# Combining expert outputs with diagonal matmuls, normalizing on ScalarE, and taking the c_fc_2 products pair by pair, in a two-layer vision kernel

## The chip, the cores and the metric

The kernel runs on one core of one Trainium2 chip. The metric is the device time of one launch in microseconds (us). It is told as the median of several runs; three runs of the kernel before gave 4483.56 us (4473.93 to 4485.39). One more execution was recorded by the hardware profiler; all durations below come from it. Engines are named as in the profile: PE is the matrix engine (PEld its weight loads), DVE the vector engine, ACT the scalar engine, POOL the general engine, SP the engine that only issues DMAs.

## The reference, cut to what matters

The input x has shape (4, 384, 32, 32): 4 batches, 384 channels, 1024 positions. All arithmetic is float32.

```python
x = x + scan_conv(ln_c(x))               # selective scan in 4 directions, then layernorm and gelu
t = tokens(x)                            # (4, 1024, 384)
t = t + experts(ln_t(t))                 # 4 experts, the best 2 for each token, weighted by their gates
x = from_tokens(t)
x = x + attention(ln_c(x))               # 8 heads of 64, output projection w_out, bias b_out
t = tokens(x)
t = t + kron_ffn(ln_t(t))                # h = gelu(n @ kron(c_fc_1, c_fc_2).T); h @ kron(c_proj_1, c_proj_2).T
...
def ln(v, eps): return (v - mean(v)) / sqrt(var(v) + eps)
out = einsum('bse,ebsd->bsd', masked_gates, y)      # the weighted sum of two experts' rows
```

kron(c_fc_1, c_fc_2) has 32 blocks of 12 channels: the product with c_fc_2 is an elementwise product of a token with a tiled row of 384 numbers, followed by a sum over each group of 12. The kernel does it before it subtracts the mean and scales, which it does on the 32 sums.

## The kernel before, in words

**Scan layer** (`scan_layer`, lines 192 to 291). For each of 4 batches there are 4 directions times 2 halves of 512 positions; each such unit has 3 chunks of 128 channels, each 4 groups of states. Per group POOL multiplies twice at L420 and once at L448 (128x1024 each), ACT makes the decays at L429, DVE runs 4 scans at L434 and 2 products at L441, and PE sums over states at L455. When a batch ends, `finish` normalizes (`layernorm`, lines 150 to 188, two halves), applies gelu and adds the input.

**Tail of a batch.** `route` and `spread` (lines 601 to 664) make tokens out of channels, take the statistics, compute gates and places (`places`), normalize each token block (L649) and scatter each row to two places in DRAM with indirect DMAs from POOL's queue (L654). `experts` (lines 807 to 902) runs 11 slots of 256 or 128 rows, each with one expert's weights: matmuls at L879, gelu at L888, matmuls at L895, an add of the bias on DVE (L899), and a DMA from SP's queue that writes the rows to `made` (L900). `combine` (lines 904 to 926) gathers for each of 8 blocks of 128 tokens the two rows `got` (L913, 16 indirect DMAs from POOL's queue), ACT multiplies each by its gate into PSUM (L920), and DVE adds both to the token block `xt` (L924). `xt` is written to DRAM (L925). `prologue` (lines 930 to 944) takes statistics (`stats`, lines 516 to 527), normalizes `xt` in place (L531), transposes on PE (L939) and copies to `xc` on ACT (L943). `attention` (lines 946 to 1047) follows, and then `last_layers` (lines 1049 to 1156): output projection (L1083) in four pairs of token blocks, added to `xt` by DVE (L1087); statistics; the product with c_fc_2 (L1091) and its sums over 12 (L1093) for all 8 blocks at once; the transposed result `z`; hidden matmuls, gelu (L1128), the second product and the output.

**Inverse roots.** In `layernorm` (L178), `stats` (L525) and `spread` (L636) ACT takes a Sqrt, `exp_again` (lines 141 to 144) loads the table of Exp and Ln back, and DVE takes the reciprocal (L180, L526, L637).

**What sets the order.** Every engine runs its instructions in the order of its queue. The order is made before the launch by a list scheduler that simulates the kernel with its own durations (line 1285); `high_priority(offset=FORWARD)` moves `combine`, `prologue`, `last_layers` and `spread` ahead of what else is ready. The tails of batches 0 and 1 and the experts of batch 2 run beside the scans of the batches after them; the rest of batch 2's tail and the whole tail of batch 3 run when the last scan has ended, at about 3555 us of the span.

**Buffers.** Tails 0 to 2 use the room `t` and batch 3 the room `w`, with the numbers of buffers per tag given here. `two()` hands out the tag "s" of PSUM (two banks), which the combine, the transposes, the hidden matmuls, the scores and the output projection share; `bank("o")` and `bank("p")` are single banks.

```python
NARROW = {"kw": 8, "k12": 2, "k4": 5, "got": 1, "bb": 2}
WIDE = {"kw": 10, "k12": 3, "k4": 4, "got": 2, "bb": 2}
NARROW_BANKS = {"s": 1, "o": 1, "p": 1}
WIDE_BANKS = {"s": 2, "o": 2, "p": 2}
```

Batch 3 has the narrow banks up to the end of `prologue`, and the wide ones from its attention on. `second_layer_exact` is inside a condition that does not hold for this input; the trace has none of its instructions.

Of the kernel before, what the change touches and what calls it, by code (L numbers as in the profile page):

```python
# [12 lines left out]
ALU = mybir.AluOpType  # L13
# [101 lines left out]
class Body:  # L115
# [29 lines left out]

    def col(self, name, i):
        at = COL[name][0] + i
        return self.cols[:, at : at + 1]

    def layernorm(self, src, dst, eps, psum, work):  # L150

        nc = self.nc
        for i in range(NH):
            sl = halves(i)
            mean = psum.tile([P, HF], F32, tag="ps", name="ln_mean")
            for c in range(DC):
# [12 lines left out]
            var = psum.tile([P, HF], F32, tag="ps", name="ln_var")  # L169
            for m in range(nm):  # L170
                for c in range(DC):
                    nc.tensor.matmul(
                        var[:, m : m + 1], sqs[c][:, m * P : (m + 1) * P], self.ones[:, :1],
                        start=(c == 0), stop=(c == DC - 1),
                    )
            std = work.tile([P, nm], F32, tag="ln_std", name="ln_std", bufs=2)
            self.exp_again(
                nc.scalar.activation(std, var[:, :nm], AF.Sqrt, bias=eps, scale=1.0 / D).ins  # L178
            )
            nc.vector.reciprocal(std, std)  # L180
# [304 lines left out]
    def first_layer(self, b, room):  # L485

        self.experts(b, self.slots, room)
        with self.tc.high_priority(offset=FORWARD):
            xt = self.combine(b, *self.place, room)
            return self.prologue(xt, xt, room)  # L490
# [25 lines left out]
    def stats(self, xt, eps, room):  # L516
# [8 lines left out]
        self.exp_again(nc.scalar.activation(rstd, mv[:, :, 1], AF.Sqrt, bias=eps).ins)  # L525
        nc.vector.reciprocal(rstd, rstd)  # L526
        return mv[:, :, 0], rstd

    def normalize(self, xt, mean, rstd, out):
        for m in range(MB):  # L530
            self.nc.vector.tensor_scalar(  # L531
                out[:, m, :], xt[:, m, :], mean[:, m : m + 1], rstd[:, m : m + 1],
                op0=ALU.subtract, op1=ALU.mult,
            )
# [71 lines left out]
    def spread(self, b, x1, room):  # L606
# [29 lines left out]
        self.exp_again(nc.scalar.activation(rstd, mv[:, :, 1], AF.Sqrt, bias=self.eps5).ins)  # L636
        nc.vector.reciprocal(rstd, rstd)  # L637
        nc.vector.tensor_mul(sc, sc, rstd.unsqueeze(2).to_broadcast([P, MB, NE]))
        nc.vector.tensor_add(sc, sc, self.bg.unsqueeze(1).to_broadcast([P, MB, NE]))
        pos, gate, expert = self.places(sc, room)  # L640
# [166 lines left out]
    def experts(self, b, routed, room):  # L807
# [57 lines left out]
        for s in range(NSLOT):  # L865
# [34 lines left out]
            nc.sync.dma_start(  # L900
# [3 lines left out]
    def combine(self, b, pos, gate, room):  # L904

        nc = self.nc
        xt = room.tile([P, MB, D], "k12", "xt")
        nc.sync.dma_start(out=xt, in_=self.tokens(b))
        got = []
# [7 lines left out]
        for m in range(MB):  # L917
            ps = room.two("w_ps")
            for k in range(TOP):
                nc.scalar.activation(  # L920
                    ps[:, k, :D], got[m][:, k, :], AF.Copy, scale=gate[:, k, m : m + 1]
                )
            for k in range(TOP):
                nc.vector.tensor_add(xt[:, m, :], xt[:, m, :], ps[:, k, :D])  # L924
        nc.sync.dma_start(out=self.tokens(b), in_=xt)  # L925
        return xt
# [3 lines left out]
    def prologue(self, xt, xn, room):  # L930

        nc = self.nc
        mean, rstd = self.stats(xt, self.eps6, room)
        self.normalize(xt, mean, rstd, xn)
        xc = room.tile([P, DC, L], "k12", "xc")
        for c in range(DC):
            ps = room.two("tc_ps")
            for m in range(MB):
                nc.tensor.transpose(  # L939
                    ps[:, m // 4, m % 4 * P : (m % 4 + 1) * P], xn[:, m, c * P : (c + 1) * P],  # L940
# [108 lines left out]
    def last_layers(self, b, att, room):  # L1049
# [27 lines left out]
        nc.gpsimd.tensor_add(xt, xt, bout.unsqueeze(1).to_broadcast([P, MB, D]))  # L1077
        for m in range(0, MB, 2):
# [8 lines left out]
            nc.vector.tensor_add(xt[:, m : m + 2, :], xt[:, m : m + 2, :], ps[:, :, :D])  # L1087

        mean, rstd = self.stats(xt, self.eps5, room)
        prod = room.tile([P, MB, D], "k12", "prod")  # L1090
        nc.vector.tensor_mul(prod, xt, c2.unsqueeze(1).to_broadcast([P, MB, D]))  # L1091
        zt = room.tile([P, MB, KR], "zt", "zt")
        nc.vector.tensor_reduce(  # L1093
            zt.rearrange("p m r -> p (m r)"), prod.rearrange("p m (r j) -> p (m r) j", j=KJ),
            AX.X, ALU.add,
        )
# [61 lines left out]
    def second_layer_exact(self):  # L1158

        nc, tc, a = self.nc, self.tc, self.a  # L1160
        with ExitStack() as ctx:
# [10 lines left out]
            for b in range(B):  # L1172
                xc = work.tile([P, DC, L], F32, tag="xc", name="xc", bufs=1)
                att = work.tile([P, HEADS // 2, L], F32, tag="att", name="att", bufs=1)
                with ExitStack() as part:
# [4 lines left out]
                    nc.vector.tensor_copy(xc, self.prologue(xt, xt, room))  # L1180
# [205 lines left out]
```

## Time and profile before

| | |
|---|---|
| median of 3 runs | 4483.56 us |
| the profiled execution's own time | 4517.48 us |
| its span, first to last instruction | 4513.6 us |
| mean granted TensorE clock | 0.831 |
| PE busy | 3440.6 us (76%) |
| DVE busy | 3010.8 us (67%) |
| POOL busy | 3037.0 us (67%) |
| ACT busy | 2534.3 us (56%) |
| 16 DMA engines, queue of SP | 50.3% |

The profile's page gives for each engine its busy share in 40 slices of the span (112.8 us each, in tenths), then the costliest groups of instructions: line, engine, operation, output<-inputs, shapes, count, busy us and mean ns, then the time that the engine stood idle just before them and what ended it. The timeline view lists instructions in order of time: start, duration, engine, line, and in brackets the idle time before and who ended it. The view by stages gives the busy time of each engine in a stretch of time.

### The profile page before, as it was taken

To read this page: it belongs to the slowest core of one execution; us is meant where nothing else is said; L and a number is where in the kernel's file an instruction comes from. 1 tells how busy PE (TensorE), PEld (TensorE's weight loads), DVE (VectorE), ACT (ScalarE), POOL (GpSimd) and SP (SyncE) were. 2 spreads that over 40 slices of the span, in tenths; PEclk is the share of its full clock that TensorE was granted. 3 is DMA by queue.
4 is the path that set the end of the run, shared out by engine and by line. 5 is a ranking of instruction groups with operands and counts; after the bars stand their busy time and mean duration, and the time that the engine had idled before them with its cause. 6 is when DMAs were issued, how large, how long until landed. Compare 5 with 4: busy or idle time off the path is not lost. (4 is left out here: it accounts for less than half of the span.)

```text
span 4513.6 us, 46925 instructions
## 1 busy us (share of the span) xinstructions
PE 3440.6 (76%) x13852; PEld 1652.0 (37%) x13852; DVE 3010.8 (67%) x4344; ACT 2534.3 (56%) x4406; POOL 3037.0 (67%) x1467
## 2 busy tenths in 40 slices
PE   6545554479894787669998588757998689999796
PEld 2111121145552222225555222214555445556333
DVE  4999997878878977977877777896778520002102
ACT  4555554456665676466666577556666444334554
POOL 4999998788987877778988778878889510000100
PEclk7666665589996898669998699858999789999897
DMA  4444554477886533457779443445787543344200
GB/s 119 118 123 118 146 136 106 137 230 209 231 240 181 149 84 104 130 159 226 210 220 275 137 114 101 115 139 170 232 244 232 169 157 115 107 127 153 75 16 15
DMA packets 404361, 684.81 MB, mean 152 GB/s; under 512 B 50944, under 2 KB 206464, under 8 KB 404096
## 3 DMA queue, kind: packets, MB, share of 16 engines
q1 hardware_dynamic: 395360, 656.16, 50.3%
q0 software_dynamic: 8192, 25.17, 1.7%
q8 instruction: 111, 1.82, 0.2%
q14 instruction: 154, 1.26, 0.1%
q10 hardware_dynamic: 544, 0.40, 0.0%
HBM read 561.47 MB, written 120.06 MB: 151 GB/s over the span
## 5 line engine op out<-in xcount | busy, mean ns | idle before, releaser
L420 POOL TENSOR_TENSOR bx<-dtr,bcs 128x1024 f32<-128x1024 f32 x768 | 1797.8, 2366 | 227.7 <-PE acc L455 103.5
L429 ACT ACTIVATE da<-dtr,nega 128x512 f32<-128x512 f32 x1536 | 1045.5, 691 | 1039.4 <-DVE bx L441 569.0
L448 POOL TENSOR_TENSOR bx<-bx,bcs 128x1024 f32<-128x1024 f32 x384 | 903.6, 2358 | 211.8 <-DVE bx L434 88.0
L455 PE MATMUL acc<-bx,sel 128*32 128x512 f32 x3072 | 511.8, 713 | 312.4 <-POOL bx L448 248.8
L879 PE MATMUL h_ps<-xc,w 128*128 128x256 f32 (+1 forms) x3168 | 680.1, 370 | 61.7 <-DVE xc L861 31.5
L895 PE MATMUL y_ps<-w,hs 128*128 128x384 f32 x1824 | 649.9, 509 | 49.8 <-ACT hs L888 44.1
L879 PEld LDWEIGHTS h_ps<-xc,w 128*128 128x128 f32 x3168 | 557.2, 200 | 253.4 <-issue 120.4
L434 DVE TENSOR_TENSOR_SCAN bx<-da,carry,bx 128x512 f32<-128x512 f32 x384 | 474.0, 1269 | 118.6 <-POOL bx L420 65.5
L434 DVE TENSOR_TENSOR_SCAN bx<-da,bx 128x512 f32<-128x512 f32 x384 | 452.2, 1209 | 129.2 <-POOL bx L420 70.3
L434 DVE TENSOR_TENSOR_SCAN da<-da,carry,bx 128x512 f32<-128x512 f32 x384 | 476.5, 1273 | 67.9 <-ACT da L429 62.6
L441 DVE TENSOR_TENSOR bx<-da,bcs 128x512 f32<-128x512 f32 x768 | 509.8, 679 | 3.8
L434 DVE TENSOR_TENSOR_SCAN da<-da,bx 128x512 f32<-128x512 f32 x384 | 456.3, 1218 | 60.7 <-ACT da L429 44.2
L895 PEld LDWEIGHTS y_ps<-w,hs 128*128 128x128 f32 x1824 | 352.3, 198 | 341.7 <-issue 86.4
L992 ACT ACTIVATE ex<-s_ps 128x512 f32<-128x512 f32 x512 | 299.4, 591 | 274.9 <-PE s_ps L987 259.9
L987 PE MATMUL s_ps<-w 64*128 64x512 f32 x1024 | 308.4, 674 | 83.1 <-ACT ex L992 74.2
L1077 POOL TENSOR_TENSOR xt<-xt,wb 128x3072 f32<-128x3072 f32 x4 | 26.8, 6708 | 477.5 <-DMA w<-in_w 345.5
L1036 PE MATMUL o_acc<-ex,vt 128*64 128x512 f32 x1024 | 295.6, 658 | 0.8 <-ACT att L1044 0.8
L455 PEld LDWEIGHTS acc<-bx,sel 128*32 128x32 f32 x3072 | 77.7, 117 | 596.0 <-POOL bx L448 363.8
L884 ACT ACTIVATE hs<-h_ps,bb 128x256 f32<-128x256 f32 (+1 forms) x528 | 194.0, 447 | 128.8 <-PE h_ps L879 128.5
L899 DVE TENSOR_TENSOR y<-y_ps,bb 128x384 f32<-128x384 f32 x76 | 41.6, 548 | 237.6 <-PE y_ps L895 237.6
L913 POOL DMA_INDIRECT got<-made,g_pos x64 | 60.8, 950 | 192.4 <-PE f_acc L1136 159.1
L987 PEld LDWEIGHTS s_ps<-w 64*128 64x128 f32 x1024 | 81.1, 192 | 266.8 <-ACT ex L992 149.1
(216 smaller groups left out, 4021.9 us busy)
## 6 DMA issues: line engine op xcount, KB each, us to landing
w<-in_w SPq DMA_DIRECT2D x352, 576.0 KB
dtr<-dd SPq DMA_DIRECT2D x1536, 128.0 KB
bcs<-rows SPq DMA_DIRECT2D x512, 128.0 KB
dd<-one_e SPq DMA_DIRECT2D x96, 256.0 KB
dd<-mag SPq DMA_DIRECT2D x96, 256.0 KB
rows<-zero SPq DMA_DIRECT2D x76, 192.0 KB
xs<-rows SPq DMA_DIRECT2D x32, 384.0 KB
made<-y SPq DMA_DIRECT2D x32, 384.0 KB
```

The costliest lines, as they stand in the source:

```text
L420: pool = nc.gpsimd.tensor_mul(bx, dtr[q][1], bc[:, 0].unsqueeze(1).to_broadcast([P, 2, HF])).ins
L429: nc.scalar.activation(da, dtr[q][0][:, j, :], AF.Exp, scale=nega[:, col : col + 1])
L434: nc.vector.tensor_tensor_scan(run(h), run(da), run(bx[:, j, :]), 0.0 if first else hold, ALU.mult, ALU.add,)
L441: dve = nc.vector.tensor_mul(bx[:, j, :], h, cg).ins
L448: pool = nc.gpsimd.tensor_mul(bx, bx, cg.unsqueeze(1).to_broadcast([P, 2, HF])).ins
L455: nc.tensor.matmul(acc[lo : lo + DB, :], sel, out[q][:, j, :], start=(g == 0), stop=(g == NG - 1),)
L879: nc.tensor.matmul(ps[:, r, :], w1[(f + r) // wf][:, c, (f + r) % wf * P : ((f + r) % wf + 1) * P], xc[:, c, :], start=(c == 0), stop=(c = ...
L884: nc.scalar.activation(hs[:, f + r, :], ps[:, r, :], AF.Identity, bias=bb[:, f + r : f + r + 1])
L895: nc.tensor.matmul(out[:, :D], hs[:, f, t * P : (t + 1) * P], w2[f // wf][:, f % wf, :], start=(f == 0), stop=(f == FC - 1),)
L987: nc.tensor.matmul(ps[:, o, :], w[rows, j * P : (j + 1) * P], w[rows, halves(i)], start=True, stop=True,)
L992: ins = nc.scalar.activation(ex[:, o, :], ps[:, o, :], AF.Exp, scale=HD**-0.5, accum_out=sums[:, t, 2 * j + o, i : i + 1],).ins
L1036: ins = nc.tensor.matmul(out[cols, :], made[t][1][:, j, cols], ex[:, o, :], start=(j == 0), stop=(j == MB - 1),).ins
```

## The change

The inverse root becomes exp(-0.5 ln(var + eps)), two ACT instructions with one table. `combine` makes two tensors of 8 diagonal matrices from the gates on POOL, and PE multiplies them with the gathered rows and sums both experts in PSUM; DVE adds a pair of blocks at once. `normalize` is gone: ACT applies scale and bias (`less` is minus mean times the inverse root) and writes, in `combine`'s case, into the first half of `got`. The last slot's rows are written to `made` from ACT's queue instead of SP's. In `last_layers` the product with c_fc_2 and its sums are taken after each pair of the output projection, with the product in the pair's PSUM tile.

```diff
+    def inverse_root(self, out, var, eps, scale=1.0):
+        self.nc.scalar.activation(out, var, AF.Ln, bias=eps, scale=scale)
+        self.nc.scalar.activation(out, out, AF.Exp, scale=-0.5)
...
# layernorm (and stats with mv[:, :, 1], eps; and spread with self.eps5)
-            self.exp_again(
-                nc.scalar.activation(std, var[:, :nm], AF.Sqrt, bias=eps, scale=1.0 / D).ins
-            )
-            nc.vector.reciprocal(std, std)
+            self.inverse_root(std, var[:, :nm], eps, scale=1.0 / D)
...
-    def normalize(self, xt, mean, rstd, out):
-        for m in range(MB):
-            self.nc.vector.tensor_scalar(
-                out[:, m, :], xt[:, m, :], mean[:, m : m + 1], rstd[:, m : m + 1],
-                op0=ALU.subtract, op1=ALU.mult,
-            )
+    def less_mean(self, mean, rstd, room, tag):
+        less = room.tile([P, MB], tag, "less")
+        self.nc.vector.scalar_tensor_tensor(less, mean, -1.0, rstd, op0=ALU.mult, op1=ALU.mult)
+        return less
...
# spread (less is taken before self.places)
-            nc.vector.tensor_scalar(
-                xt[:, m % 2, :], xt[:, m % 2, :], mv[:, m, :1], rstd[:, m : m + 1],
-                op0=ALU.subtract, op1=ALU.mult,
+            nc.scalar.activation(
+                xt[:, m % 2, :], xt[:, m % 2, :], AF.Identity,
+                bias=less[:, m : m + 1], scale=rstd[:, m : m + 1],
             )
...
# experts
-            nc.sync.dma_start(
+            queue = nc.sync if s + 1 < NSLOT else nc.scalar
+            queue.dma_start(
                 out=made[at : at + size, :].rearrange("(t p) d -> p t d", p=P), in_=y
             )
...
# combine
+        diag = []
+        for k in range(TOP):
+            d = room.tile([P, MB, P], "k4", "diag")
+            nc.gpsimd.tensor_mul(
+                d, self.ident.unsqueeze(1).to_broadcast([P, MB, P]),
+                gate[:, k, :].unsqueeze(2).to_broadcast([P, MB, P]),
+            )
+            diag.append(d)
...
-        for m in range(MB):
+        for m in range(0, MB, 2):
             ps = room.two("w_ps")
-            for k in range(TOP):
-                nc.scalar.activation(
-                    ps[:, k, :D], got[m][:, k, :], AF.Copy, scale=gate[:, k, m : m + 1]
-                )
-            for k in range(TOP):
-                nc.vector.tensor_add(xt[:, m, :], xt[:, m, :], ps[:, k, :D])
+            for o in range(2):
+                for k in range(TOP):
+                    nc.tensor.matmul(
+                        ps[:, o, :D], diag[k][:, m + o, :], got[m + o][:, k, :],
+                        start=(k == 0), stop=(k == TOP - 1),
+                    )
+            nc.vector.tensor_add(xt[:, m : m + 2, :], xt[:, m : m + 2, :], ps[:, :, :D])
         nc.sync.dma_start(out=self.tokens(b), in_=xt)
-        return xt
+        return xt, [got[m][:, 0, :] for m in range(MB)]
...
# prologue
         mean, rstd = self.stats(xt, self.eps6, room)
-        self.normalize(xt, mean, rstd, xn)
+        less = self.less_mean(mean, rstd, room, "less")
+        for m in range(MB):
+            nc.scalar.activation(
+                xn[m], xt[:, m, :], AF.Identity, bias=less[:, m : m + 1], scale=rstd[:, m : m + 1]
+            )
...
# last_layers, after each pair of the output projection
+            pair = xt[:, m : m + 2, :]
+            nc.vector.tensor_add(pair, pair, ps[:, :, :D])
+            nc.vector.tensor_mul(ps[:, :, :D], pair, c2.unsqueeze(1).to_broadcast([P, 2, D]))
+            for o in range(2):
+                nc.vector.tensor_reduce(
+                    zt[:, m + o, :], ps[:, o, :D].rearrange("p (r j) -> p r j", j=KJ),
+                    AX.X, ALU.add,
+                )
         mean, rstd = self.stats(xt, self.eps5, room)
-        prod = room.tile([P, MB, D], "k12", "prod")
-        nc.vector.tensor_mul(prod, xt, c2.unsqueeze(1).to_broadcast([P, MB, D]))
...
-        nc.vector.tensor_reduce(
-            zt.rearrange("p m r -> p (m r)"), prod.rearrange("p m (r j) -> p (m r) j", j=KJ),
-            AX.X, ALU.add,
-        )
```

More of the change, by code (lines that the diff above doesn't have):

```diff
@@ L488, in first_layer @@
         with self.tc.high_priority(offset=FORWARD):
-            xt = self.combine(b, *self.place, room)
-            return self.prologue(xt, xt, room)
+            xt, xn = self.combine(b, *self.place, room)
+            return self.prologue(xt, xn, room)
     def second_layer(self, b, xc, room, between):
@@ L524, in stats @@
             nc.vector.bn_aggr(mv[:, m, :], st[:, m, :])
-        self.exp_again(nc.scalar.activation(rstd, mv[:, :, 1], AF.Sqrt, bias=eps).ins)
-        nc.vector.reciprocal(rstd, rstd)
+        self.inverse_root(rstd, mv[:, :, 1], eps)
         return mv[:, :, 0], rstd
-    def normalize(self, xt, mean, rstd, out):
-        for m in range(MB):
-            self.nc.vector.tensor_scalar(
-                out[:, m, :], xt[:, m, :], mean[:, m : m + 1], rstd[:, m : m + 1],
-                op0=ALU.subtract, op1=ALU.mult,
-            )
+    def less_mean(self, mean, rstd, room, tag):
+        less = room.tile([P, MB], tag, "less")
+        self.nc.vector.scalar_tensor_tensor(less, mean, -1.0, rstd, op0=ALU.mult, op1=ALU.mult)
+        return less
     def moe_consts(self, room):
@@ L635, in spread @@
             nc.sync.dma_start(out=self.tokens(b)[:, m : m + 2, :], in_=xt)
-        self.exp_again(nc.scalar.activation(rstd, mv[:, :, 1], AF.Sqrt, bias=self.eps5).ins)
-        nc.vector.reciprocal(rstd, rstd)
+        self.inverse_root(rstd, mv[:, :, 1], self.eps5)
         nc.vector.tensor_mul(sc, sc, rstd.unsqueeze(2).to_broadcast([P, MB, NE]))
         nc.vector.tensor_add(sc, sc, self.bg.unsqueeze(1).to_broadcast([P, MB, NE]))
+        less = self.less_mean(mv[:, :, 0], rstd, room, "r_less")
         pos, gate, expert = self.places(sc, room)
@@ L939, in prologue @@
                 nc.tensor.transpose(
-                    ps[:, m // 4, m % 4 * P : (m % 4 + 1) * P], xn[:, m, c * P : (c + 1) * P],
+                    ps[:, m // 4, m % 4 * P : (m % 4 + 1) * P], xn[m][:, c * P : (c + 1) * P],
                     self.ident,
@@ L1077, in last_layers @@
         nc.gpsimd.tensor_add(xt, xt, bout.unsqueeze(1).to_broadcast([P, MB, D]))
+        zt = room.tile([P, MB, KR], "zt", "zt")
         for m in range(0, MB, 2):
@@ L1086, in last_layers @@
                     )
-            nc.vector.tensor_add(xt[:, m : m + 2, :], xt[:, m : m + 2, :], ps[:, :, :D])
-        mean, rstd = self.stats(xt, self.eps5, room)
-        prod = room.tile([P, MB, D], "k12", "prod")
-        nc.vector.tensor_mul(prod, xt, c2.unsqueeze(1).to_broadcast([P, MB, D]))
-        zt = room.tile([P, MB, KR], "zt", "zt")
-        nc.vector.tensor_reduce(
-            zt.rearrange("p m r -> p (m r)"), prod.rearrange("p m (r j) -> p (m r) j", j=KJ),
-            AX.X, ALU.add,
-        )
+            pair = xt[:, m : m + 2, :]
[6 more added lines that the diff above has]
+                )
+        mean, rstd = self.stats(xt, self.eps5, room)
         shift = room.tile([P, MB], "shift", "shift")
@@ L1179, in second_layer_exact @@
                     nc.sync.dma_start(out=xt, in_=self.tokens(b))
-                    nc.vector.tensor_copy(xc, self.prologue(xt, xt, room))
+                    xn = [xt[:, m, :] for m in range(MB)]
+                    nc.vector.tensor_copy(xc, self.prologue(xt, xn, room))
                 with ExitStack() as part:
```

## The prediction

> **What bounds the kernel now.** I read the profile's page first, the engines' busy share in 40 slices:
>
> ```profile
> PE   6545554479894787669998588757998689999796
> DVE  4999997878878977977877777896778520002102
> ...
> POOL 4999998788987877778988778878889510000100
> ```
>
> Up to slice 31 (about 3550 us) DVE and POOL run the scan, nearly full while nothing else runs (slices 1 to 5) and at 7 to 9 tenths once the tails run beside it. Then both fall idle and PE works alone. So there are two limits. The groups say why POOL and DVE are so close:
>
> ```profile
> L420 POOL TENSOR_TENSOR bx<-dtr,bcs 128x1024 f32<-128x1024 f32 x768 | 1797.8, 2366 | 227.7 <-PE acc L455 103.5
> ...
> L448 POOL TENSOR_TENSOR bx<-bx,bcs 128x1024 f32<-128x1024 f32 x384 | 903.6, 2358 | 211.8 <-DVE bx L434 88.0
> ```
>
> Per group of states POOL has 3 such instructions, 7.1 us; DVE has four scans of 1.24 us and two products of 0.68 us, 6.3 us, plus copies and its share of the tails. Neither is the limit alone; what the tails put on DVE comes back in part.
>
> For the part after the scan I read the timeline, since the chain of waits reaches back only to 3043 us. The view by stages of the two combines there (batch 2 beside the scan's last layernorm, batch 3 before its attention), with columns PE, PEld, DVE, ACT, POOL, clock, DMA, shows that no engine is full in either:
>
> ```profile
> 3553.00:3609.00 56.00, 21.71 (x83) 16.29 (x82) 24.34 (x54) 27.57 (x36) 22.56 (x22) 0.57 0.49 154
> 4184.00:4249.00 65.00, 38.62 (x184) 20.89 (x184) 20.05 (x44) 34.67 (x40) 15.20 (x16) 0.72 0.40 124
> ```
>
> They are chains of waits. The timeline of batch 3's:
>
> ```profile
> 4208.38 0.95 POOL L913 DMA_INDIRECT got<-made,g_pos  x1 [0.30 <-issue]
> ...
> 4213.89 1.14 DVE L924 TENSOR_TENSOR xt<-xt,w_ps 128x384 f32<-128x384 f32 x2 [11.47 <-ACT w_ps L920]
> ...
> 4231.50 1.14 DVE L924 TENSOR_TENSOR xt<-xt,w_ps 128x384 f32<-128x384 f32 x2 [0.46 <-ACT w_ps L920]
> ...
> 4238.43 3.20 DVE L531 TENSOR_SCALAR xt<-xt,mv,rstd 128x384 f32<-128x384 f32 x8 [2.35 <-DMA x<-xt]
> ```
>
> The last gather is issued at 4209.33, but the last add ends at 4232.64: one PSUM tile goes back and forth between ACT and DVE, and ACT's queue also holds the copies and gelus of batch 2's last layers. Then the normalization waits 2.35 us because it overwrites a tile that a DMA still reads.
>
> At the end, DVE alone, with PE idle 10.9 us:
>
> ```profile
> 4439.10 3.34 DVE L1091 TENSOR_TENSOR prod<-xt,wb 128x3072 f32<-128x3072 f32 x1
> ...
> 4442.51 3.32 DVE L1093 TENSOR_REDUCE zt<-prod 128x256 f32<-128x3072 f32 x1
> ...
> 4446.47 1.43 DVE L1102 TENSOR_TENSOR z<-zt,rstd 128x256 f32<-128x256 f32 x4
> ```
>
> **The change part by part.** All of it stands against this profiled execution (4517.48 us, span 4513.6), which is 34 us above the median of the three runs; I take the difference off the median.
>
> *Scan stage, DVE* (occurrences before 3550 us). Gone: 32 adds of L924 at 0.55 (17.7 us); the normalizations L531 of batches 0 and 1 (11.4 + 5.2 us; undisturbed they take 3.2 each) and L649 of batches 0 to 2 (30.4 less 3.4 of batch 3, 27.0 us); the product and sums L1091 and L1093 of batches 0 and 1 (30.6 less 13.3 of the others, 17.3 us); some 21 reciprocals (4 us). Sum 82.6 us. New: 8 adds of 768 at 0.95 (row L1087), 7.6; 8 products of 768 into PSUM at about 0.95 (same row), 7.6; 16 sums of 384 at 0.48 (L1093: 3.32 us for 3072, so 0.415 for 384, plus some 0.06 of start), 7.7; 5 `less` at 0.2 (row L638), 1.0. Sum 23.9 us. DVE gets 58 us lighter (82.6 less 23.9 is 58.7).
>
> L531 and L649 are long only in the scan stage: eight took 11.41 us at 1443 us, of which one alone 8.69, while POOL ran three products in a row, against 0.40 each at 4238. The new product also has both inputs in SBUF: L1102, another such, took 2.55 us for four at 1878 us and 1.43 at 4446, and L638 took 2.34 beside POOL and 0.19 without it. So each of the 8 products may wait 0 to 2.2 us, at most 17 us in all; I take 3, since L1102's four lost about 1.1 us together.
>
> The Trainium skill ("SBUF — State Buffer", section "Who interferes with whom") states this as a lock: a DVE instruction with two SBUF inputs, or in a 2-port mode as a tensor_scalar can be, blocks fully against a POOL instruction that reads SBUF, and a reduction never does. It speaks for moving L531 and L649 and against cutting one product into four, since each piece can meet the lock; by the rule the pieces cost up to 17 us, by the row about 3.
>
> *Scan stage, ACT.* 21 Sqrts go, each with a table load before and after: 42 x 1.283 = 53.9 us, and 5.8 us for themselves; 32 products L920 at 0.58, 18.7 us. New: 21 times Ln at 0.3 (a 128x8 Sqrt takes 0.30) and Exp at 0.23 (row of 128x32), 11 us; 40 normalizations of 384 at about 0.6 (L920 with one pointer operand 0.58; L362 with 512 columns 0.72), 24 us. ACT gets 43 us lighter. It isn't the limit, but DVE's scans waited 212 us for its decays.
>
> The Trainium skill ("ScalarE: Activation LUTs", section "What ACT_TABLE_LOAD costs") puts a switch at about 2.66 us, with a drain behind the load. Here the drain does not show: at 4234.24 a load of 1.28 us is followed by its Sqrt at 4235.54. By the rule ACT would gain some 58 us more; I stay with the row.
>
> *Scan stage, POOL.* Two diagonal products per batch, 128x1024 from two SBUF inputs: 2.36 us each by L420, 6 of them, 14.2 us on a queue that is nearly the limit; bounds 0 (if they land in one of POOL's waits) and 14. They sit in its queue before the gathers and need two "k4" buffers of the last expert slots; if the queue gets to them early, the products behind them wait.
>
> *Scan stage, PE.* 16 products of 384 columns per batch; L895's records take 0.51 us, two each, so 16 us a batch, which lie under the gathers (16 issues, 1.25 us apart, 20 us).
>
> Sum for the scan stage: DVE 58 less 3, of which I count half since POOL stands beside it (-28), POOL +14: **-14 us**. Ends: all of DVE's and nothing of POOL's, -58; nothing of DVE's, all of POOL's and of the lock, +31.
>
> *Combine of batch 2* (3553 to 3609). The last gather is issued by 3576.0 and lands 2.2 us later (the first of batch 3 is issued by 4188.76 and used at 4190.94). Then one product (1.0), one add (0.95) and two statistics (1.5) end at 3581.7; now they end at 3602.0. The inverse root is 0.7 us instead of 0.3 + 0.2, but without loads; the normalization starts at once instead of 5.5 us later, since it writes another tile, and takes 8 x 0.6 = 4.8 instead of 3.2 us. `xc` is 23 us earlier. What that is worth: from 3700 us PE is full to 4184 with experts of batch 3 and attention of batch 2; the lead pays only where PE is idle, and between 3600 and 3700 it is busy 77.5 us. So 0 to 22 us; I take half, **-11 us**. In the last layernorm (L178) the load already hides behind the variance matmuls: nothing there.
>
> *Combine of batch 3.* In the same way the statistics end at 4215, not 4233.5, and `xc` is some 21 us earlier. But batch 2's last layers share PE and ACT, hold the narrow banks until their output (4240.5) and, at the same gather times, need about 7 us for a hidden block, 4 for its gelu, twice, 4 for the product and 8 for the output from 4187, so 4223 at best. Ends 0 and -21; I take **-15 us**, as ACT loses the 16 products between them.
>
> *Last layers of batch 3.* Per pair PE takes 5.16 us; DVE's add, product, two sums and statistics take 0.95 + 0.95 + 0.96 + 1.3 = 4.2 us, so three pairs hide. After the last add (4438.1) come 3.2 us, then 0.6 of mean and shift: z starts at 4442.1, not 4446.5: **-4 us** (-3 to -5). The cover is PE's; with one bank, as in batches 0 to 2, the pair's tile is held about 2 us longer, but there PE has experts to run.
>
> *The last write of `made` from ACT's queue.* In batches 0, 2 and 3 SP issued it 0.02 to 0.03 us after the add, so nothing is gained. ACT must wait for that add: behind it stand the scan's decays. An issue on ACT took 0.45 us (L203). Ends 0 and +4 (a bias add's wait of some us in each batch); I take 0.
>
> Sum: 14 + 11 + 15 + 4 = 44 us off 4483.56: **4440 us**.
>
> **The rivals.**
> *All of it couples* (chance 0.08): DVE's 55 us and both leads of 21 come through: -58 - 22 - 21 - 5 = -106 at the extreme, some -90 likely, 4394. For it: DVE and ACT wait for each other 917 us at L429. Against: POOL's own 2702 us.
> *The leads are not used* (0.17): batch 2's last layers hold batch 3, and PE's idle time is waiting for `places`, not for `xc`. Only 14 + 4 remain: 4465. For it: POOL waited 56.2 us for the places before the scatter.
> *POOL decides the scan* (0.12): the diagonals cost 14, DVE's relief nothing; with half the leads, +14 - 13 - 4 = -3: 4480, no change.
> *PE's queue takes over the wait* (0.15): a combine's matmul waits for its gather at the head of PE's queue, and behind it stand the scan's sums L455, the last layernorm's matmuls and batch 2's hidden blocks. First issue to last landing is 23.7 us (4187.8 to 4211.5). Held for 20 us in batches 0, 1 and 2, and batch 3's lead lost, it costs 60 against 14 + 11 + 4: +31, 4515. It decides from about 10 us per combine (three of them against 29). For it: POOL already waited 103.5 us for L455. Against: POOL issues gathers for 20 us in that stretch and feeds the scan nothing, so PE has little to do.
>
> **How the numbers follow.** The forecast's own case has 0.48. A measurement here tells 0.3%, 13 us, from no change. Faster: 0.48 + 0.08 + 0.17 = 0.73; same 0.12; slower 0.15. The range 4400 to 4490 leaves out most of the first and of the last rival, about 0.19. All queues are laid out anew by a planner; that may add either sign, and is why I keep the range this wide.
>
> **What would show it.** Right: the last add of batch 3's combine within 5 us of its last landing; no table load at Sqrt; L649's and L531's place taken by ACT at 0.55 to 0.65 us each; z within 5 us of the last pair's add; the scan's end some 14 us earlier than 3550. Wrong: PE idle on gathers with L455 or L172 behind; POOL waiting at the diagonals; the scan's end later than now.

## The result, and the profile after

The changed kernel took 4527.01 us (median of four runs, 4524.48 to 4532.37), the kernel before on the same chip 4478.75 us (4472.73 to 4485.39). The ratio is 1.0109, 95% interval 1.0089 to 1.0129: slower by about 48 us, and above the predicted range. The profiled execution took 4532.37 us, its span is 4530.6 us, the mean granted clock 0.842.

The page of the changed kernel, the same three engines in 40 slices:

```profile
PE   5554554549997888669998687768999699999797
DVE  4888888778887866978886766888788730020002
...
POOL 3899988778898867788998766879899821000100
```

In slices 1 to 5 (113 to 680 us), where nothing but the scan of batch 0 runs, DVE has fallen from 9 to 8 tenths, and POOL shows two 8s where it had only 9. Both engines do the same scan work there, so something makes them wait. POOL's costliest groups (busy, mean, idle before and what ended it):

```profile
L422 POOL TENSOR_TENSOR bx<-dtr,bcs 128x1024 f32<-128x1024 f32 x768 | 1794.4, 2362 | 270.4 <-PE acc L457 145.7
...
L450 POOL TENSOR_TENSOR bx<-bx,bcs 128x1024 f32<-128x1024 f32 x384 | 904.3, 2359 | 243.6 <-DVE carry L447 108.0
```

They are as long as before, and the idle time ahead of them is larger, 514.0 us instead of 439.5. The reason stands in ACT's groups for the first 900 us. First the kernel before:

```profile
L144 ACT ACT_TABLE_LOAD x8 | 10.3, 1283 | 0.1
L178 ACT ACT_TABLE_LOAD x6 | 7.7, 1283 | 4.6 <-PE ln_var L172 4.6
...
L636 ACT ACT_TABLE_LOAD x1 | 1.3, 1283 | 0.0
```

Then the changed kernel:

```profile
L355 ACT ACT_TABLE_LOAD x27 | 34.6, 1283 | 4.2 <-DMA dd<-one_e 3.3 <-PE dt_ps L360 0.4
L431 ACT ACT_TABLE_LOAD x25 | 32.1, 1283 | 0.4
L148 ACT ACT_TABLE_LOAD x6 | 7.7, 1283 | 4.6 <-PE ln_var L177 4.6
L149 ACT ACT_TABLE_LOAD x6 | 7.7, 1283 | 0.1
L353 ACT ACT_TABLE_LOAD x2 | 2.6, 1283 | 0.0
```

With the single loads of both lists, 69 loads now against 17 before. L355 is the scan's Ln and L431 its Exp: lines that the diff does not touch. ACT's timeline of the changed kernel (start, duration) shows how they take the table from each other:

```profile
308.90 1.28 ACT L355 ACT_TABLE_LOAD   x1
310.19 0.63 ACT L355 ACTIVATE lnw<-one_e 128x512 f32<-128x512 f32 x1
310.85 0.63 ACT L357 ACTIVATE one_e<-one_e 128x512 f32<-128x512 f32 x1
311.50 1.28 ACT L431 ACT_TABLE_LOAD   x1
312.79 1.30 ACT L431 ACTIVATE da<-dtr,nega 128x512 f32<-128x512 f32 x2
```

In the kernel before, `exp_again` stood behind each Sqrt, and the first of them, in batch 0's first layernorm, loaded the set of tables that holds Exp and Ln together. The change removes it there. ACT's timeline of the kernel before, then of the changed kernel, at that place:

```profile
19.70 1.28 ACT L178 ACT_TABLE_LOAD   x1 [4.56 <-PE ln_var L172]
21.00 0.26 ACT L178 ACTIVATE ln_std<-ln_var,eps 128x4 f32<-128x4 f32 x1
21.28 1.28 ACT L144 ACT_TABLE_LOAD   x1
```

```profile
19.93 1.28 ACT L148 ACT_TABLE_LOAD   x1 [4.56 <-PE ln_var L177]
21.22 0.26 ACT L148 ACTIVATE ln_std<-ln_var,eps 128x4 f32<-128x4 f32 x1
21.51 1.28 ACT L149 ACT_TABLE_LOAD   x1
22.80 0.20 ACT L149 ACTIVATE ln_std<-ln_std 128x4 f32<-128x4 f32 x1
```

L144 is `exp_again`; L148 and L149 are the Ln and the Exp of the new root. Nothing else asks for that set before the `exp_again` behind the first gelu, at 853 us; until then each Ln and each Exp is given a set that lacks the other. Start of the scan layer's gelu, batch by batch:

| | batch 0 | 1 | 2 | 3 | span |
|---|---|---|---|---|---|
| before | 791 | 1731 | 2674 | 3592 | 4513.6 |
| after | 849 | 1788 | 2756 | 3683 | 4530.6 |
| after, with one load of the joint set at the start (the first run below) | 789 | 1728 | 2695 | 3616 | 4464.2 |

58 us are lost before the first gelu. Against the third row, 60 us are lost there and 66 at the end: they are not won back. Against the kernel before, the distance grows to 91 us at batch 3 and shrinks to 17 at the end: from the scan's last sum to the end it takes 878 us instead of 960, and the profiled execution of the kernel before was a long one, 34 us above its median. What the change promised for the combine is there too. The changed kernel's timeline of DVE, end of batch 3's combine (the last gather is issued by about 4250):

```profile
4253.35 0.95 DVE L937 TENSOR_TENSOR xt<-xt,w_ps 128x768 f32<-128x768 f32 x1 [2.14 <-PE w_ps L933]
4254.34 1.02 DVE L525 BATCH_NORM_STATS2 st<-xt 128x6 f32<-128x384 f32 x2
4255.28 0.30 DVE L526 BATCH_NORM_AGGREGATE mv<-st 128x2 f32<-128x6 f32 x2
4256.19 0.17 DVE L533 SCALAR_TENSOR_TENSOR less<-mv,rstd 128x8 f32<-128x8 f32 x1 [0.61 <-ACT rstd L149]
```

The last add ends 4.9 us after the last gather's start; it was 24.3. And batch 3's last pair of the output projection:

```profile
4458.88 0.95 DVE L1107 TENSOR_TENSOR xt<-xt,o_ps 128x768 f32<-128x768 f32 x1 [1.21 <-PE o_ps L1102]
...
4463.67 1.43 DVE L1121 TENSOR_TENSOR z<-zt,rstd 128x256 f32<-128x256 f32 x4
```

`z` starts 3.8 us after the last add ends, where it was 8.3.

### The profile page after: what moved, and what is told of

The parts are those of the page before. It is cut to its first block, busy times and chain, and to the rows that moved or that the text cites. A ratio compares the mean times of both kernels' runs of the same rounds, so it can differ in the third digit from the quotient of the medians.

```text
span 4530.6 us, 47195 instructions
## 1 busy us (share of the span) xinstructions
PE 3496.9 (77%) x13980; PEld 1660.7 (37%) x13980; DVE 2977.3 (66%) x4252; ACT 2555.5 (56%) x4446; POOL 3051.1 (67%) x1475
## 5 line engine op out<-in xcount | busy, mean ns | idle before, releaser
L422 POOL TENSOR_TENSOR bx<-dtr,bcs 128x1024 f32<-128x1024 f32 x768 | 1794.4, 2362 | 270.4 <-PE acc L457 145.7
L431 ACT ACTIVATE da<-dtr,nega 128x512 f32<-128x512 f32 x1536 | 1044.3, 690 | 1046.2 <-DVE bx L443 610.3
L879 PE MATMUL h_ps<-xc,w 128*128 128x256 f32 (+1 forms) x3168 | 669.3, 366 | 50.4 <-DVE xc L861 25.8
L916 POOL TENSOR_TENSOR diag<-ident,g_picked 128x1024 f32<-128x1024 f32 x8 | 15.0, 1894 | 274.3 <-DMA out<-out 261.1
L347 PE MATMUL dt_ps<-xd,wdt 12*128 12x512 f32 x192 | 127.2, 747 | 69.0 <-ACT mag L386 31.6
```

What stands on the lines that cost most here:

```text
L422: pool = nc.gpsimd.tensor_mul(bx, dtr[q][1], bc[:, 0].unsqueeze(1).to_broadcast([P, 2, HF])).ins
L431: nc.scalar.activation(da, dtr[q][0][:, j, :], AF.Exp, scale=nega[:, col : col + 1])
L879: nc.tensor.matmul(ps[:, r, :], w1[(f + r) // wf][:, c, (f + r) % wf * P : ((f + r) % wf + 1) * P], xc[:, c, :], start=(c == 0), stop=(c = ...
```

## The experiments

Each run is told as a ratio to runs of the kernel before that were made beside it, since the kernel before itself took 4479.6, 4511.3, 4477.7 and 4513.9 us beside the four groups of runs, the last two on the same chip. Letters in the expectations: T, the table loads cost what was lost, against R, the other parts did; P, each part has the price that its own instructions show, against Q, the order of the queues decides; W, the wait for `less`, against O, the order. The expectations also call PE TensorE, DVE VectorE, ACT ScalarE and POOL GpSimd. Line numbers shift a little from kernel to kernel.

**First group: the tables.** One line added to the changed kernel, `e1_after_preload`:

```diff
-            nc.scalar.activation(nega, self.cols[:, lo:hi], AF.Exp)
+            self.exp_again(nc.scalar.activation(nega, self.cols[:, lo:hi], AF.Exp).ins)
```

> The changed kernel with one table load more: right behind the first Exp (nega) the table that holds both Exp and Ln is loaded. Theory T (tables): in batch 0 no instruction loads that table any more, so Ln and Exp take it from each other some 50 times up to 850 us; with the load the loads at L353, L355 and L431 vanish, the first gelu of the scan layer comes back from 846 us to about 790 us, and the kernel takes 4465 to 4485 us, level with the kernel before (4479) or below it. Rival R (DVE's waits for POOL at the small products and the new order): at most 10 us come back, over 4515 us.

Measured 4466.19 us, ratio 0.997 (0.9958 to 0.9981), 61 us under the changed kernel. Its loads in the first 900 us are four, of which the joint set is loaded at L144:

```profile
L144 ACT ACT_TABLE_LOAD x2 | 2.6, 1283 | 0.0
L208 ACT ACT_TABLE_LOAD x1 | 1.3, 1283 | 1.7 <-PEq L1397 1.7
L230 ACT ACT_TABLE_LOAD x1 | 1.3, 1283 | 0.0
```

The queues of PE, DVE, POOL and SP hold the same instructions in the same order in both kernels, and ACT's differ by loads only: a clean pair, two kernels whose queues are the same but for the part in question. T holds.

`e2_root_only`: the kernel before with only the inverse root changed. `e3_root_preload`: the same with the line above.

```diff
-            self.exp_again(
-                nc.scalar.activation(std, var[:, :nm], AF.Sqrt, bias=eps, scale=1.0 / D).ins
-            )
-            nc.vector.reciprocal(std, std)
+            self.inverse_root(std, var[:, :nm], eps, scale=1.0 / D)
...
```

> The kernel before with the inverse root alone changed to Ln and Exp (three places), without a preload. T: the same 50 loads in batch 0, first gelu at about 840 us, 4520 to 4540 us. R: the roots alone take table loads and reciprocals away, 4460 to 4480 us.

> The kernel before with the inverse root alone changed, and the shared table loaded behind the first Exp. T: no load in batch 0's scan but one, 56 loads fewer than before: 4455 to 4478 us. R: the same as e2 within 10 us.

Measured 4550.82 us, 1.0163 (1.0146 to 1.018), somewhat above T's range, and 4498.09 us, 1.0033 (1.002 to 1.0045). Again the two kernels' queues differ by loads alone, 65 of them, and the difference is 53 us. So T's mechanism shows twice, at 53 and 61 us for 83.4 us of loads. But without the extra loads the new root is not faster than Sqrt and reciprocal, although 55 loads fewer than before are in the trace: T's 4455 to 4478 for the second was wrong.

`e4_all_but_root`: the changed kernel with Sqrt, `exp_again` and the reciprocal back.

```diff
-        self.inverse_root(rstd, mv[:, :, 1], eps)
+        self.exp_again(nc.scalar.activation(rstd, mv[:, :, 1], AF.Sqrt, bias=eps).ins)
+        nc.vector.reciprocal(rstd, rstd)
...
```

> The changed kernel with the old Sqrt, table loads and reciprocals put back; combine by TensorE, normalization by ScalarE, pair products and the queue of the last write stay. T: no loads of Ln against Exp in batch 0; what is left of the change gains at most the leads of the two late combines: 4445 to 4480 us. R: these parts are what costs, over 4500 us.

Measured 4513.03 us, 1.0066 (1.0049 to 1.0083), with 17 loads in the first 900 us. That is above T's 4445 to 4480 and inside R's range: the rest of the change without the new root was slower than the kernel before too. The clean pairs rule R out for the 61 us, but the other parts were not free.

**Second group: one part back at a time, from the version with the preload (0.997).**

`e5_sync_write` issues the last `made` write from SP again; `e6_no_pairs` takes the products with c_fc_2 at once; `e7_dve_normalize` has both normalizations on DVE and no `less`; `e8_old_combine` has the combine of the kernel before.

```diff
# e5_sync_write
-            queue = nc.sync if s + 1 < NSLOT else nc.scalar
-            queue.dma_start(
+            nc.sync.dma_start(
# e6_no_pairs, and the products and sums of the kernel before behind the statistics
-            pair = xt[:, m : m + 2, :]
-            nc.vector.tensor_add(pair, pair, ps[:, :, :D])
-            nc.vector.tensor_mul(ps[:, :, :D], pair, c2.unsqueeze(1).to_broadcast([P, 2, D]))
+            nc.vector.tensor_add(xt[:, m : m + 2, :], xt[:, m : m + 2, :], ps[:, :, :D])
...
# e7_dve_normalize, both places
-            nc.scalar.activation(
-                xn[m], xt[:, m, :], AF.Identity, bias=less[:, m : m + 1], scale=rstd[:, m : m + 1]
+            nc.vector.tensor_scalar(
+                xn[m], xt[:, m, :], mean[:, m : m + 1], rstd[:, m : m + 1],
+                op0=ALU.subtract, op1=ALU.mult,
# e8_old_combine, and without the diagonals
+                nc.scalar.activation(
+                    ps[:, k, :D], got[m][:, k, :], AF.Copy, scale=gate[:, k, m : m + 1]
+                )
+            for k in range(TOP):
+                nc.vector.tensor_add(xt[:, m, :], xt[:, m, :], ps[:, k, :D])
...
```

> As e1 (the changed kernel with the shared table loaded early), but the last slot's rows go to made from SP's queue again. Theory P (the parts are worth what the prediction priced): 0, so 4463 to 4470 us. Rival Q (each edit lays all queues anew, and the new order is worth more than the part): off e1's 4466 by more than 8 us, either way.

> As e1, with the product and sums with c_fc_2 for all 8 blocks at once again. P: the last batch's z comes 4 us later and the scan is unchanged within 5 us: 4468 to 4476 us. Q: off that by more than 8 us, either way; z of the last batch is 4 us later behind the last add in any case.

> As e1, with the two normalizations by VectorE again (the combine's one still writes another tile). P: 44 us of VectorE come back in the scan stage, half of it counts: 4480 to 4495 us; single instructions of 2 us and more beside GpSimd show again at that line. Q: less than 8 us, or faster than e1.

> As e1, with the old combine (ScalarE times the gate, VectorE adds), so no diagonals on GpSimd. P: both late combines again end 20 us behind their last gather, the scan loses 10 us of VectorE and gains 14 of GpSimd: 4480 to 4495 us. Q: less than 8 us, or faster than e1.

Measured: 0.9963 (0.9951 to 0.9975), 0.9951 (0.9934 to 0.9968), 0.9911 (0.9887 to 0.9934), 0.9962 (0.9951 to 0.9973). The queue of the write, the pairs and even the combine on PE can be taken out and nothing is lost; giving the normalizations back to DVE gained 0.6%, where a loss was expected. Taken as ratios, P's range holds for `e5_sync_write` alone. That one is nearly a clean pair: besides the moved DMA issues two PE instructions change places. For the other three the scheduler lays the queues anew.

**Third group: why the normalizations on ACT cost.** The groups had one odd row: `less`, 128x8 elements, took between 152 and 12671 ns in the version with the preload, and ACT waited for it 29.2 us ahead of the eight normalizations that follow the combine. Its durations there (shortest, median, longest), and below them those of `e11_less_from_psum`:

```profile
L533 DVE SCALAR_TENSOR_TENSOR less<-mv,rstd x8: 152/1256/12671, 847.2 to 4189.8; 128x8 f32<-128x8 f32 x8
L535 DVE SCALAR_TENSOR_TENSOR less<-mv,l_ps x8: 135/157/165, 842.7 to 4150.3; 128x8 f32<-128x8 f32 x8
```

`e9_dve_before_projections` and `e10_dve_before_scatters` give one of the two places back to DVE, with the edit of `e7_dve_normalize`; `e11_less_from_psum` keeps both on ACT and changes where `less` reads:

```diff
         less = room.tile([P, MB], tag, "less")
-        self.nc.vector.scalar_tensor_tensor(less, mean, -1.0, rstd, op0=ALU.mult, op1=ALU.mult)
+        ps = room.bank("p", "l_ps")
+        self.nc.scalar.copy(ps[:, :MB], rstd)
+        self.nc.vector.scalar_tensor_tensor(
+            less, mean, -1.0, ps[:, :MB], op0=ALU.mult, op1=ALU.mult
+        )
```

`e12_dve_both_no_pairs` is `e7_dve_normalize` with the products at once.

> The changed kernel with the preload, and only the normalization ahead of the projections (after the combine) back on VectorE, without its `less`; the one ahead of the scatters stays on ScalarE. With the preload alone the ratio to the kernel before was 0.997, with both normalizations on VectorE 0.9911: 0.59%, some 26 us, to divide. Theory W, that the cost is the wait for `less` and the eight normalizations behind it between a batch's combine and its projections (28 us of ScalarE's waits in four batches, of which the last batch's are on the end's path, 4 to 8 us, and the others delay what stands behind them on ScalarE): this run gets most of it back, ratio 0.990 to 0.993. Theory O, that the gain came from another order of the queues that the scheduler laid with the lighter ScalarE: no division to be had, this run and the next lie anywhere between 0.989 and 0.999, and their gains do not add to 0.59%.

> The mirror of the run before: with the preload, only the normalization ahead of the scatters back on VectorE, without its `less`; the one after the combine stays on ScalarE. W: little comes back, ratio 0.995 to 0.998. O: anywhere between 0.989 and 0.999, and the two runs' gains do not add to 0.59%.

> The changed kernel with the preload, both normalizations on ScalarE, but `less` reads the inverse root from a PSUM bank (one more ScalarE copy of 128x8, 0.2 us a place, and a bank of the shared ones), so that VectorE's instruction has one input in SBUF. If `less` waits for the port that POOL holds (152 ns the shortest, 12671 ns the longest with the same operands), its mean falls from some 3.6 us to under 0.5 us; W then says that most of ScalarE's 29 us of waits go and the ratio falls to 0.992 to 0.995. If the waits stand at other things (the queue of VectorE in front of `less`), its mean stays over 2 us. O: ratio 0.995 to 0.999 even where the mean falls.

> Both normalizations on VectorE, the preload, and the products with c_fc_2 at once as in the kernel before: what is left of the change is the inverse root, the combine on TensorE and the made-write. With the preload alone, the pairs taken away gave 0.9951 against 0.997, and the normalizations taken back 0.9911. If the parts add, 0.989; if the pairs' 4 us in the last batch are real and only the order differed there, 0.991 to 0.993; theory O allows 0.988 to 0.997.

Measured: 0.9993 (0.9977 to 1.0009), 1.0093 (1.0072 to 1.0114), 0.9888 (0.987 to 0.9907) and 1.003 (1.0018 to 1.0042). The gain of `e7_dve_normalize` does not divide: half of it is no gain in one place (0.2% slower than none, intervals overlapping) and 1.2% slower than none in the other. W's division is refuted: the gains do not add, as O said. But O's ranges do not hold either, since `e10_dve_before_scatters` and `e12_dve_both_no_pairs` lie above them; what made these two slow is open. `e11_less_from_psum` is better than W said: all eight `less` take 135 to 165 ns, and it is the fastest so far.

**Fourth group: a control, and two parts priced again without the wait.** `e13_less_control` keeps the copy to PSUM and lets `less` read `rstd` from SBUF again:

```diff
-            less, mean, -1.0, ps[:, :MB], op0=ALU.mult, op1=ALU.mult
+            less, mean, -1.0, rstd, op0=ALU.mult, op1=ALU.mult
```

> The kernel of the run before that had `less` reading PSUM, with the same additional copies of the inverse root to a PSUM bank, but `less` reading the SBUF tile again. W: the three waits of 6 to 13 us are back, the projections of the first three batches start 12 to 15 us after the combine's last add instead of 3 to 5, and the ratio is that of the preload alone, 0.996 to 0.999, against 0.9888. If the copies or the bank had made the difference, it stays at 0.987 to 0.991. It isn't a pure pair: the scheduler lays VectorE's and POOL's queues here as in the preload alone, and otherwise with `less` from PSUM.

Measured 0.9969 (0.9958 to 0.998), as with the preload alone: the copies and the bank are worth nothing. What gives the 0.8% is the operand, together with the order of the queues that the scheduler lays with it. Up to batch 0's combine the queues of this run and of `e11_less_from_psum` are the same but for one neighbour of the first `less`, so the two timelines can be laid side by side there. DVE in the control, then POOL in the control:

```profile
1408.62 7.27 DVE L535 SCALAR_TENSOR_TENSOR less<-mv,rstd 128x8 f32<-128x8 f32 x1 [0.61 <-ACT rstd L149]
1415.82 2.45 DVE L436 TENSOR_TENSOR_SCAN bx<-da,carry,bx 128x512 f32<-128x512 f32 x2
```

```profile
1403.11 6.95 POOL L422 TENSOR_TENSOR bx<-dtr,bcs 128x1024 f32<-128x1024 f32 x3
1410.03 1.25 POOL L378 TENSOR_TENSOR lnw<-lnw,mag 128x512 f32<-128x512 f32 x1
1411.25 4.62 POOL L422 TENSOR_TENSOR bx<-dtr,bcs 128x1024 f32<-128x1024 f32 x2
1418.41 2.35 POOL L450 TENSOR_TENSOR bx<-bx,bcs 128x1024 f32<-128x1024 f32 x1 [2.54 <-DVE bx L436]
```

DVE with `less` from PSUM:

```profile
1398.69 0.17 DVE L535 SCALAR_TENSOR_TENSOR less<-mv,l_ps 128x8 f32<-128x8 f32 x1 [0.81 <-ACT l_ps L534]
1398.77 2.45 DVE L436 TENSOR_TENSOR_SCAN bx<-da,carry,bx 128x512 f32<-128x512 f32 x2
```

In the control `less` starts while POOL runs products back to back, and ends at 1415.89, within 0.02 us of the end of POOL's last one at 1415.87. DVE's scans stand behind it, POOL's next product waits for them, and ACT's normalizations wait for `less`: the transposes start 10 us after the last add, against 3 us. With the preload alone the same `less` started at 1400.80, took 12.67 us and ended with POOL's run, too (1413.47 and 1413.44).

The expectation was off in its sizes. In batches 0 to 2 `less` took 7.3, 3.2 and 3.4 us in the control, not 6 to 13, and the transposes started 10, 13 and 10 us after the last add. But counted from the start of the last gather they start 20, 23 and 20 us later in the control as with the preload alone, and 8, 11 and 9 us later with `less` from PSUM.

From add to transposes the version with the preload took 15, 15, 15 and 3 us in the four batches, with `less` from PSUM it was 3, 6, 3 and 3. The three differences add up to 34 us, near the 36.3 us between their spans, but that proves nothing: at the gelus of batches 1, 2 and 3 `e11_less_from_psum` is 27, 13 and 13 us ahead, not 12, 21 and 34. So the wait is shown, and that the operand ends it; how much of the 36 us it is, and how much the order of the queues, is not settled.

`e14_psum_old_combine` and `e15_psum_no_pairs` are `e11_less_from_psum` with the old combine and with the products at once:

> The changed kernel with the preload and `less` from PSUM (0.9888), with the combine of the kernel before: products by ScalarE, sums by VectorE, no diagonals on POOL. The gathers of the last batch to the last add take 25 us there against 4 to 5 us after the last gather here, and 19 to 21 us against 10 to 15 in the other batches. My combine terms (26 us in all) say a ratio of 0.992 to 0.996. Rival O: the combine's part is lost in another order of the queues, 0.986 to 0.991.

> The changed kernel with the preload and `less` from PSUM (0.9888), with the products with c_fc_2 at once behind the layernorm's sums. Locally 4 us in the last batch are lost: 0.989 to 0.991 if nothing else moves. Rival O: the three other batches' queues are laid anew and the ratio lies anywhere between 0.984 and 0.995.

Measured 1.0008 (0.9998 to 1.0018), above both ranges, and 0.9863 (0.9845 to 0.9881). The version with the combine on PE is 1.2% faster here, more than my 26 us, after it had gained nothing over `e8_old_combine`. Its own instructions do not explain that: from the start of the last gather to the end of the last add it takes 5.4, 4.9, 6.1 and 5.0 us, the old one there 8.6, 9.4, 9.1 and 12.7, 18 us together. The delay grows along the way: with the old combine batch 0's gathers start 8 us later, its transposes 18, its output projection is added 45 us later (1796 against 1751) and batch 1's scatters start 59 us later (1931 against 1872). From the transposes on, attention and the next batch's tail run beside the scan in queues that were laid in another order. Part of these distances is none of the kernels' doing, since the two traces come from groups beside which the kernel before itself differed by 36 us. How much of it is the combine and how much the order I have not settled. The pairs' intervals overlap with those of the version that has them: nothing to be seen of their 4 us in the time, though they are there locally: `z` starts 3.8 us after the last add with the pairs and 8.4 us after it in `e15_psum_no_pairs`.

`e15_psum_no_pairs` and `e11_less_from_psum` beat both kernels, by 1.1 to 1.4% against before.

## Why the prediction was wrong, step by step

- **Scan stage, ACT: the step that failed.** The forecast said that 21 Sqrts go, "each with a table load before and after", 42 loads less, made ACT 43 us lighter and put that at nothing in the sum ("It isn't the limit"). It counted the loads that belong to the Sqrts and did not ask what the ones behind them were for. One of them gave batch 0's Ln and Exp their common set. In place of 42 loads less ahead of 3550 us, the trace has 24 more there (155 against 131) and 12 more in all (197 against 185). In the first 900 us it has 52 more, where ACT's decays feed a DVE and a POOL that are nearly full. "No table load at Sqrt" came true to the letter and hid the point: Ln and Exp of the new root have loads of their own (L148, L149). Measured: 61 us in the changed kernel, where the sum had 0. With the joint set loaded once the count comes out as forecast (90 loads ahead of 3550 us, 41 less).
- The Trainium skill ("ScalarE: Activation LUTs", section "Table sets: the hidden batching unit") says that Ln followed by Exp is one load, since one set has both. This trace disagrees: that holds only while that set is loaded, and so does the "one table" in the description of the change; 27 loads at L355 and 25 at L431 are what was put in where it was not.
- **Scan stage, DVE: `less` at 0.2 us was mis-sized.** It is 0.15 us where POOL does not hold it up and up to 12.7 us beside POOL, 29.2 us for the eight of the changed kernel. I had read the lock for the new products, gave them 3 us of it in the scan stage, and missed the small operand that stands in front of ACT's eight normalizations. Against `less` from PSUM it gave back 9 to 12 us of each lead but the last batch's. The version without it is 36 us faster, but its queues are laid otherwise too. The row that priced the lock was too kind: L1102 at 1878 us lost 1.1 us, but at 2975 us, in the same trace, two of its four took 2.56 us each. And the normalization of 8.69 us at 1443 us looks like the same wait: it ended 0.2 us after POOL's run of products. The products of the pairs were mis-sized as well: 0.97 us each where POOL stood still, up to 3.12 us beside its products, mean 1471 ns instead of 950, 8 us over all sixteen.
- **The weight of the scan stage's terms.** `e3_root_preload` has 55 loads less than before and gained nothing, 0.33% the other way. DVE's 58 us, counted half, never showed as an earlier end of the scan: its last sum ended at 3554 us before, at 3653 in the changed kernel, at 3588 with the preload and at 3571 with `less` from PSUM. Part of that is work of batch 2's tail that moved ahead of the scan's end, so the stage cannot be priced by itself, and my split at 3550 us was not a stage border that stays in place.
- **POOL's diagonals** were 1.89 us each, not 2.36. The rival that PE's queue takes over the wait is present in part: POOL's wait for PE's sums went from 103.5 to 145.7 us, and is still 123.4 us in the kernel that gains 1.1%, so it doesn't decide.
- **Combine of batch 3**: right. Last add 4.9 us after the last gather's start, transposes 23 us closer to the gather than before (I said 21). ACT's normalization took 0.69 us, not 0.6.
- **Combine of batch 2**: the add is 21 us closer to the gather, as said; `less` ahead of the normalization took most of it back, the transposes started 15 us behind the add, against 7 before.
- **Last layers of batch 3**: right, 4.5 us closer. At 0.1% it can't be seen in the time.
- **The write of `made` from ACT's queue at 0**: right, 0.9963 against 0.997, intervals overlapping.
- **The range.** I named the planner as a reason to keep it wide and still gave it no size. Beside the version with the preload, a small edit together with the new order of the queues moved the time by anything from 0.8% less to 1.2% more. The slow rivals were of another kind than what happened: none of them was a resource that the removed code had been setting up.

With both hidden costs removed the change gives 0.9888 of the time before, about 50 us, near the 44 us of the forecast. That agreement is of the total only: the terms behind it are not confirmed one by one.

## What to carry to other kernels

Before an instruction is removed, ask what state it leaves behind for lines that the diff does not touch (here, the table set that the scan's Ln and Exp share), and look for the first place that would set it again. A tiny instruction is priced by what can hold it up, not by its size: read the longest of its kind, and give it an operand that doesn't meet the lock where another engine's queue waits for it. And where a scheduler lays the queues, price a part only by pairs whose queues are the same but for that part; otherwise what the order does, here up to about 1%, is put down to the edit.

## What the runs showed of the hardware that I had not expected

- Two functions that have a common table set still load 1283 ns each, time and again, if that set isn't the one in place: 65 loads, 83.4 us of ACT, cost 53 and 61 us of the kernel's time in two clean pairs. No gap follows a load in the timeline above: the Exp starts at 312.79, 0.01 us after it.
- A product of 128x8 on DVE with two operands in SBUF took 7.27 us beside POOL's products, across the borders of several of them, until POOL paused; 12.67 us at the longest. With one operand in PSUM it took 135 to 165 ns in 24 of 24 cases. The Trainium skill ("SBUF — State Buffer", section "Who interferes with whom") states that such an instruction contends with a POOL instruction that reads SBUF, and says of the modes that use both ports that who issues first holds them for the whole instruction; that the wait goes on over POOL's next instructions is what these rows add. It does not always: batch 0's `less` ahead of the scatters, in the changed kernel, took 2.35 us and ended at 909.43 with one product of POOL, whose next product followed without a pause. When it gets in and when not, no run here shows. DVE, then POOL:

```profile
907.08 2.35 DVE L533 SCALAR_TENSOR_TENSOR less<-mv,rstd 128x8 f32<-128x8 f32 x1
```

```profile
904.75 6.96 POOL L422 TENSOR_TENSOR bx<-dtr,bcs 128x1024 f32<-128x1024 f32 x3
911.65 2.36 POOL L450 TENSOR_TENSOR bx<-bx,bcs 128x1024 f32<-128x1024 f32 x1
```
